# Three seams of a fused graph-convolution and attention kernel: column sums before transposes, extra matmuls at attention's beginning, and two more partial sums on TensorE at its end

## The chip, the cores and the metric

The kernel runs on one core of a Trainium2 chip. Times are device microseconds (us) of a whole execution. The engines are named as in the profile: PE is TensorE's matrix multiplications, PEld its weight loads, DVE is VectorE, ACT is ScalarE, POOL is GpSimd, and SP is the engine that issues most DMAs. "L341" is line 341 of the kernel before.

## The reference

Inputs are `x` (8 graphs x 2048 nodes x 256 features, f32) and one adjacency matrix `adj` (2048 x 2048, f32, with many zeros). Two layers follow each other:

```python
# layer 0: graph convolution, two linear maps, each with a batch norm; residual; layer norm
A = adj + eye
deg  = A.sum(0) + A.sum(1) - diagonal(A)
dinv = rsqrt(deg)
A_hat = A * dinv[:, None] * dinv[None, :]
agg = einsum('nm,bmd->bnd', A_hat, x).reshape(-1, 256)
h   = relu(batchnorm(agg @ W1.T + b1))          # 512 wide, over all 16384 rows
y   = batchnorm(h @ W2.T + b2)                  # 256 wide
x   = layernorm(x + y)
# layer 1: masked attention with 4 heads of 64; residual; layer norm
q, k, v = split(x @ W)
s    = q @ k.T / 8, with -inf where adj == 0
x    = layernorm(x + softmax(s) @ v)
```

All arithmetic stays in f32.

## The kernel before, in words

**Stage 1** reads the adjacency in 16 row tiles `a` of 128 x 2048, in a fixed order of tiles; three buffers hold them. For each tile, PE transposes its sixteen 128 x 128 blocks, four to a PSUM tile `ps` (L234, four buffers); DVE moves three of the four PSUM tiles into the transposed matrix `T` (L240) and ACT the fourth (L238). PE also adds the tile's columns into the PSUM tile `pc` by matrix products with ones (L244), ACT sums its rows (L242), DVE takes its diagonal (L223), and POOL marks the zeros of the diagonal block and adds the identity to it (L249, L250). After the last tile, ACT copies `pc` to `cs` (L261), PE turns `cs` (L264), DVE adds the row and the column sums (L265, L268), and POOL raises the degrees to the power -1/2 in four instructions of four columns each (L99), which gives `dinv`. DVE then makes the first difference of quarters of `T` (`first_t1`, L216 and L217). In this stage DVE, POOL and SP keep the order of the program text (`manual_schedule`); PE and ACT are placed by a planner. In every later stage but a short one all the engines keep the order of the text.

**The first layer.** Products with `T` are made by a recursive scheme with seven products of quarters (`p1` to `p7`) per unit. Each product is eight f32 matrix multiplications, two instructions each (L341). ACT first scales the features of the first unit by `dinv` (L317, 32 instructions), in the order of the halves (0,0), (1,0), (1,1), (0,1); `p1` reads the first, `p2` the last. Then come the linear maps and batch norms (lines 380 to 700).

**Attention's beginning.** The first graph's four chunks of 512 rows get the last batch norm on ACT (`bn`, L764). `ready(c)` transposes such a chunk on PE in two halves into one PSUM tile (`turn_y`, L779, four transposes each); DVE adds the residual (`add_y`, L787) and takes the layer norm's statistics (L728, L730), and POOL makes the roots (`root`, L97, L99, L735, L736). ACT applies the norm (L740), PE turns the result (`turn`, L808), ACT copies it out (L814), and PE projects it to keys and queries (`project`, L845) and values (L859).

**Attention proper.** There are NU = 64 units (a graph, a pair of heads, a chunk of 512 queries) of NT = 16 steps, one for each 128 keys. At step g, PE makes the scores of step g + 3 (L910), DVE masks them (L922), ACT takes the exponential (L928), and PE multiplies those of step g with the values (`weigh`, L940). The softmax's denominators need the sum of all 16 probability tiles `prob` of a unit: POOL adds odd steps to even ones by accumulating DMAs (L950), adds the pairs into `acc` on its own ALU (L959 and L961, five steps after the pair), and PE sums `acc` over its partitions with ones (`finish_sums`, L977). In the last unit the steps 12 to 15 are left to PE as four further `parts`. Small tasks are hung on steps by `at_step(u, j, ...)`: a whole number j runs ahead of the masking of that step, a fraction after it. When the last step is done, what hangs on units NU and NU + 1 runs in order: `finish_sums`, a copy to `sm` (L985), a transpose of it (`finish_turn_sums`, L991, L993, L998), a transpose of the output (`finish_turn`, L1004), the weighting and residual (`finish`, L1012), the final layer norm by halves and the stores (L824). `count_sums` (L1022 to L1028) counts how many of the 8 x 64 sums of each partition are in range; a branch after it (L1255) recomputes everything another way if one is not.

Of the kernel before, what the change touches and what calls it, by code (L numbers as in the profile page):

```python
# [8 lines left out]
F32 = mybir.dt.float32  # L9
U8 = mybir.dt.uint8  # L10
AF = mybir.ActivationFunctionType
ALU = mybir.AluOpType
# [10 lines left out]
SUM_MAX = 1e30  # L23
# [3 lines left out]
def tile_gcn_then_masked_attention(  # L27
# [15 lines left out]
    nc = tc.nc  # L43
    ENG = mybir.EngineType
    PSUM = bass.MemoryType.PSUM
    P = 128
# [8 lines left out]
    CH = 512  # L55
# [142 lines left out]
    with tc.tile_pool(name="bt7", bufs=1, side="right") as bp7, tc.tile_pool(  # L198
        name="stage", bufs=2, side="right"
    ) as sp, tc.tile_pool(name="stage1", bufs=1, side="right") as sp1, tc.tile_pool(  # L200
        name="pst", bufs=4, space=PSUM
    ) as pst, tc.tile_pool(name="psc", bufs=1, space=PSUM) as psc, tc.manual_schedule(
        engines={ENG.SP, ENG.Pool, ENG.DVE}
    ):
        T[1, HALVES[3]] = quarter(7, bp7)
        m8 = bp.tile([P, HT, CH], U8, name="m8")
        rsum = sp1.tile([P, NT], F32, name="rsum")
        diag = sp1.tile([P, NT], F32, name="diag")

        pc = psc.tile([P, CH], F32, name="pc")  # L210
        order = [j * HT + (NK - 1) * TPC + q for j in range(2) for q in range(TPC)]
        order += [j * HT + q for q in range(TPC) for j in range(2)]

        def first_t1(engine, here):
            t1 = T[0, (0, 1)][:, :, here]
            engine.tensor_scalar(m8[:, :, here], t1, 0.0, None, op0=ALU.is_equal)  # L216
            engine.tensor_sub(t1, t1, T[0, (0, 0)][:, :, here])  # L217

        for n, t in enumerate(order):
            a = sp.tile([P, N], F32, name="a", bufs=3)  # L220
            nc.sync.dma_start(a, adj[t * P : (t + 1) * P, :])
# [8 lines left out]
            for g in range(NT // 4):  # L230
# [6 lines left out]
                if g == NT // 4 - 1:  # L237
# [3 lines left out]
            junk = sp1.tile([P, N], U8, name="junk")  # L241
            nc.scalar.activation(junk, a, AF.Copy, accum_out=rsum[:, t : t + 1])  # L242
            for c in range(NCH):
                nc.tensor.matmul(  # L244
                    pc[32 * c : 32 * (c + 1), :], ones[:, :32], a[:, c * CH : (c + 1) * CH],
                    start=(n == 0), stop=(n == NT - 1),
                )
            ad = T[k, (j, j)][:, m, here]
            nc.gpsimd.tensor_scalar(mdiag[:, t, :], ad, 0.0, None, op0=ALU.is_equal)  # L249
            nc.gpsimd.tensor_add(ad, ad, ident)  # L250
            if k == 0 and j == 1 and q < 2:
                first_t1(nc.gpsimd, here)
        for i, j in HALVES:
            S[0, i, j] = load_form(i, j, 0)
        nc.sync.dma_start(w1s, w1t.rearrange("(c p) f -> p c f", p=P))
        for t, src in params:
            nc.sync.dma_start(t, src)
# [3 lines left out]
        nc.scalar.copy(cs, pc)  # L261
# [6 lines left out]
        nc.vector.tensor_add(  # L268
            rsum.rearrange("p (j i) -> p i j", i=TPC),
            pt.rearrange("p i (j r) -> p i j r", j=NCH)[:, :, :, 0],  # L270
            rsum.rearrange("p (j i) -> p i j", i=TPC),
        )
        for q in range(NT // 4):
            qs = slice(q * 4, (q + 1) * 4)
            rsqrt(dinv[:, qs], rsum[:, qs], 4, 0.0)
        first_t1(nc.vector, slice(2 * P, CH))
        mask_out(0, (0, 1), m8)

# [598 lines left out]
    def attention():  # L877


        with tc.tile_pool(  # L880
# [12 lines left out]

            PAIRS = range(0, NT - 2, 2)

            def on_pe(u):
# [46 lines left out]
            def add_up(g):  # L945

                u, j = divmod(g, NT)
                here = NT - on_pe(u)
                if j - 1 in PAIRS and j < here:
                    nc.gpsimd.dma_start(probs[g - 1], probs[g], accum_op=ALU.add)  # L950
                elif PAIRS[-1] + 1 < j < here:
                    nc.gpsimd.tensor_add(accs[u], accs[u], probs[g])  # L952

                v, i = divmod(g - 5, NT)
                if v < 0 or i not in PAIRS[1:] or i + 1 >= NT - on_pe(v):
                    return
                if i == PAIRS[1]:
                    accs[v] = ap_.tile([P, 2, CH], F32, name="acc")
                    nc.gpsimd.tensor_add(accs[v], probs[g - 7], probs[g - 5])  # L959
                else:  # L960
                    nc.gpsimd.tensor_add(accs[v], accs[v], probs[g - 5])  # L961
# [6 lines left out]
            def finish_sums(u):  # L968

                pm = ps_m.tile([P, BR], F32, name="pm")  # L970
                parts = [probs.pop(g) for g in range((u + 1) * NT - on_pe(u), (u + 1) * NT)]
                parts.append(accs.pop(u))
                for n, part in enumerate(parts):
                    for h in range(2):
                        for q in range(2):
                            r0 = 32 * (2 * h + q)
                            nc.tensor.matmul(  # L977
                                pm[r0 : r0 + 32, :], ones[:, :32],
                                part[:, h, q * BR : (q + 1) * BR],
                                start=(n == 0), stop=(n == len(parts) - 1),  # L980
                            )
# [3 lines left out]
                nc.scalar.copy(sts[u], pm)  # L985
# [28 lines left out]
                            op0=ALU.mult, op1=ALU.add,  # L1014
                        )

            def count_sums():

                flat = sums_all.rearrange("p u t h -> p (u t h)")
                ok = ap_.tile([P, CH], F32, name="ot")  # L1020
                cnt = ap_.tile([P, 1], F32, name="cnt", bufs=1)
                nc.vector.tensor_scalar(ok, flat, SUM_MIN, None, op0=ALU.is_ge)  # L1022
                nc.vector.scalar_tensor_tensor(
                    ok, flat, SUM_MAX, ok, op0=ALU.is_le, op1=ALU.mult, accum_out=cnt
                )
                pm = ps_m.tile([1, 1], F32, name="pm")
                nc.tensor.matmul(pm, cnt, ones[:, :1], start=True, stop=True)
# [16 lines left out]
            for u in range(NU):  # L1044
# [11 lines left out]
                elif u == NU - 1:  # L1056
                    for half in range(2):
                        at_step(u + 1, 10.4 + half, inp.emit_stats, b, c, half)
                        at_step(u + 1, 10.5 + half, inp.root_half, b, c, half)
                        at_step(u + 1, 12 + half, inp.emit_half, b, c, half)  # L1060
                    at_step(u + 1, 14, count_sums)
                elif hp == HP - 1:
                    for half in range(2):
                        at_step(u + 1, 12.5 + 1.5 * half, inp.emit_stats, b, c, half)
# [46 lines left out]
            with tc.manual_schedule(engines=IN_ORDER):  # L1111
                for c in range(NCH):
                    inp.yt[0, c] = y0[c]
                    inp.x1[0, c] = ip.tile([P, TPC, D], F32, name="x1", bufs=NCH + 4)
                    for o in range(NO):
                        inp.bn(0, c, o)

                def ready(c):
                    pm = ps_s.tile([P, TPC, D], F32, name="st")
                    for half in range(2):  # L1120
                        pmh = pm[:, half * IT : (half + 1) * IT, :]
                        inp.turn_y(0, c, half, pmh)
                        inp.add_y(0, c, half, pmh, x0[c])
                    inp.root(0, c)

                def halves(f, c):
                    for half in range(2):
                        f(0, c, half)

                for c in range(NCH - 1):  # L1130
                    ready(c)
                halves(inp.apply, 0)
# [168 lines left out]
```

## Time and profile before

| | |
|---|---|
| median of three runs | 3573.38 us (3570.64 to 3573.6) |
| the profiled execution's own time | 3573.89 us |
| its span, first to last instruction | 3571.8 us |
| PE busy | 3524.8 us (99%) |
| POOL busy | 2335.5 us (65%) |
| DVE busy | 2112.7 us (59%) |
| ACT busy | 1575.7 us (44%) |
| mean granted TensorE clock | 0.994 |

The busy times are of one profiled execution. PE is busy in 3524.8 of 3571.8 us, so all its pauses together are 47.0 us; a pause elsewhere that doesn't lengthen one of these, or the time after the last product, is hidden. The granted clock is the speed that TensorE was allowed, 1.0 or 0.5 of the full one in this trace; the records call a slow multiplication just as busy as a fast one.

### The profile page before, as it was taken

The numbers are of one execution on the slowest core, as the hardware profiler recorded it, in microseconds if no ns is written. First come the engines' busy times: TensorE is split into PE (matmuls) and PEld (weight loads), VectorE is DVE, ScalarE is ACT, GpSimd is POOL, SyncE is SP. The second block draws the span as 40 slices with busy tenths as digits, with TensorE's granted clock in tenths as the row PEclk, the third lists the DMA queues.
The fourth block names the chain that finished last, engine by engine and source line by source line (L and its number), as shares of the span: only waits on it lengthen the run. The fifth ranks groups of instructions, "written<-read, shape, count | busy, mean of one in ns | idle before, by whom it ended". The sixth has DMA issues, their size and how long they took to land. (4 is left out here: it accounts for less than half of the span.)

```text
span 3571.8 us, 55309 instructions
## 1 busy us (share of the span) xinstructions
PE 3524.8 (99%) x22447; PEld 1461.9 (41%) x22447; DVE 2112.7 (59%) x3125; ACT 1575.7 (44%) x1952; POOL 2335.5 (65%) x1590
## 2 busy tenths in 40 slices
PE   8999999999999899999999999999999999999997
PEld 5444444444444433433343433343443334343332
DVE  6224342432356656766766776676676676676666
ACT  5000000000045455665665565565566565566555
POOL 4544364435357556777777787777677777777777
PEclk9999999999999899999999999999999999999999
DMA  9122242231256445666575566566556556655555
GB/s 342 53 77 81 90 159 71 71 100 41 77 228 241 152 83 108 129 126 123 111 149 117 115 130 134 110 137 129 114 124 142 110 122 137 120 114 122 113 113 114
DMA packets 197577, 440.16 MB, mean 123 GB/s; under 512 B 14128, under 2 KB 121152, under 8 KB 186944
## 3 DMA queue, kind: packets, MB, share of 16 engines
q0 software_dynamic: 64656, 239.37, 35.3%
q1 hardware_dynamic: 132048, 196.11, 16.0%
q8 instruction: 178, 2.92, 0.3%
q10 hardware_dynamic: 608, 1.06, 0.1%
q14 instruction: 87, 0.71, 0.1%
HBM read 126.62 MB, written 75.51 MB: 57 GB/s over the span
## 5 line engine op out<-in xcount | busy, mean ns | idle before, releaser
L922 DVE SCALAR_TENSOR_TENSOR prob<-mask,st 128x1024 f32<-128x1024 uint8 x1024 | 1239.1, 1215 | 434.5 <-PE st L910 360.6
L928 ACT ACTIVATE prob<-prob 128x1024 f32<-128x1024 f32 x1024 | 1081.2, 1056 | 913.5 <-DVE prob L922 836.3
L940 PE MATMUL out_ps<-prob,v 64*64 64x512 f32 x8192 | 1075.0, 595 | 3.6 <-DVE ot L966 2.6
L910 PE MATMUL st<-qt,kt 64*64 64x512 f32 x8192 | 1063.6, 589 | 0.1
L961 POOL TENSOR_TENSOR acc<-acc,prob 128x1024 f32<-128x1024 f32 x319 | 830.0, 2602 | 5.7 <-DMA prob<-prob 0.7
L341 PE MATMUL pa<-t,x 128*128 128x512 f32 x1792 | 774.5, 594 | 2.7 <-ACT x L317 2.7
L950 POOL DMA_DIRECT2D prob<-prob x447 | 403.8, 929 | 565.3 <-PE out_ps L940 458.0
L910 PEld LDWEIGHTS st<-qt,kt 64*64 64x64 f32 x8192 | 312.6, 133 | 566.7 <-issue 526.9
L341 PEld LDWEIGHTS pa<-t,x 128*128 128x128 f32 x1792 | 342.1, 191 | 431.9 <-issue 427.7
L940 PEld LDWEIGHTS out_ps<-prob,v 64*64 64x64 f32 x8192 | 290.9, 133 | 542.1 <-issue 469.4
L952 POOL TENSOR_TENSOR acc<-acc,prob 128x1024 f32<-128x1024 f32 x126 | 298.1, 2365 | 7.5
L845 PE MATMUL pm<-x1t,wq 128*128 128x512 f32 x512 | 253.0, 617 | 0.7 <-ACT x1t L814 0.7
L470 POOL TENSOR_TENSOR ag<-ag,dbc 128x512 f32<-128x512 f32 x16 | 20.2, 1263 | 314.5 <-DVE ag L469 287.9
L450 ACT COPY ag<-pa 128x512 f32<-128x512 f32 x16 | 9.4, 588 | 448.2 <-PE pa L341 435.1
L399 ACT COPY h<-ph 128x512 f32<-128x512 f32 x28 | 16.4, 585 | 416.7 <-PE ph L390 416.7
L959 POOL TENSOR_TENSOR acc<-prob 128x1024 f32<-128x1024 f32 x64 | 171.1, 2674 | 3.0 <-DMA prob<-prob 3.0
L740 ACT ACTIVATE x<-x,ln_nm,ln_rs 128x256 f32<-128x256 f32 x256 | 137.6, 586 | 8.7 <-POOL ln_nm L736 8.7
L845 PEld LDWEIGHTS pm<-x1t,wq 128*128 128x128 f32 x512 | 87.9, 191 | 119.5 <-issue 112.8
L1012 DVE SCALAR_TENSOR_TENSOR x<-pm,ri,x 128x64 f32<-128x64 f32 x512 | 109.5, 277 | 44.1 <-PE pm L1004 44.1
L859 PE MATMUL pm<-wq,x1t 128*128 128x128 f32 x1024 | 125.1, 276 | 0.0
L859 PEld LDWEIGHTS pm<-wq,x1t 128*128 128x128 f32 x1024 | 119.4, 192 | 2.5 <-ACT x1t L814 1.7
L966 DVE TENSOR_TENSOR ot<-out_ps,ot 128x512 f32<-128x512 f32 x64 | 44.3, 692 | 124.4 <-ACT ot L965 124.4
(156 smaller groups left out, 2855.8 us busy)
## 6 DMA issues: line engine op xcount, KB each, us to landing
prob<-prob POOLq DMA_DIRECT2D x447, 512.0 KB, 4.9
x<-in_x_dram SPq DMA_DIRECT2D x92, 512.0 KB, 6.6
h_d<-h SPq DMA_DIRECT2D x28, 1024.0 KB, 4.2
t<-h_d SPq DMA_DIRECT2D x28, 1024.0 KB, 7.5
a<-in_adj_dram SPq DMA_DIRECT2D x16, 1024.0 KB, 5.0
y_d<-ag SPq DMA_DIRECT2D x32, 512.0 KB, 2.6
out_dram<-x SPq DMA_DIRECT2D x31, 512.0 KB, 6.8
yt<-y_d SPq DMA_DIRECT2D x28, 512.0 KB, 3.2
```

The costliest lines, as they stand in the source:

```text
L341: nc.tensor.matmul(pa, s.t[:, m, :], t[:, m, :], start=(m == 0), stop=(m == HT - 1))
L740: nc.scalar.activation(self.t[:, i, :], self.t[:, i, :], AF.Identity, bias=self.nm[:, i : i + 1], scale=self.rs[:, i : i + 1],)
L845: nc.tensor.matmul(pm, wq[:, d, wcols], xt[:, d, cols], start=(d == 0), stop=(d == ND - 1))
L859: nc.tensor.matmul(pm[:, j * P : (j + 1) * P], xt[:, d, t * P : (t + 1) * P], wq[:, d, wcols], start=(d == 0), stop=(d == ND - 1),)
L910: nc.tensor.matmul(st[r * HD : (r + 1) * HD, h, :], kt[hs, j * P + r * HD : j * P + (r + 1) * HD], qt[hs, cols], start=True, stop=True,)
L922: nc.vector.scalar_tensor_tensor(p, mask[:, j, cols][:, None, :].to_broadcast([P, 2, CH]), MASKED, st, op0=ALU.mult, op1=ALU.add,)
L928: nc.scalar.activation(probs[g], probs[g], AF.Exp)
L940: nc.tensor.matmul(outs[u][hs, r, :], inp.qkv[b, hp][2][rs, j, hs], probs[g][rs, h, :], start=(j == 0), stop=(j == NT - 1),)
L950: nc.gpsimd.dma_start(probs[g - 1], probs[g], accum_op=ALU.add)
L952: nc.gpsimd.tensor_add(accs[u], accs[u], probs[g])
L959: nc.gpsimd.tensor_add(accs[v], probs[g - 7], probs[g - 5])
L961: nc.gpsimd.tensor_add(accs[v], accs[v], probs[g - 5])
```

## The change

It has four parts.

1. **Stage 1.** PE and ACT now keep the order of the text too. The body of the loop is cut into helpers (`turn_a`, `diagonal`, `sum_rows`, `sum_columns`) that hold the same instructions. For the last of the 16 tiles the loop stops after `sum_rows`: its column sums come first, then DVE instead of ACT copies `pc` to `cs`, two of its four groups of transposes stand ahead of the transposes of `cs`, and the other two, with `diagonal`, after the powers. Of the four groups, DVE moves the first and the third, ACT the second and the fourth.
2. **Attention's beginning.** A helper `warm(n)` issues n matrix multiplications of 128 x 512 on PE whose results are not read. Five stand ahead of the first `ready`; one more follows each half's transposes for the chunks 0 and 1.
3. **The last unit's sums.** POOL no longer adds the pairs at steps 8 and 10 into `acc`; PE sums them as two more `parts`, and `acc` is now the first of the parts, not the last.
4. **The range count.** It is made in two: the sums of units 0 to 62 in step 12 of the last unit, the last unit's own after its sums are known. PE adds the two counts with two multiplications, and that (`count_bad`) now stands between the statistics and the root of the first half of the last chunk.

```diff
@@ stage 1
-        engines={ENG.SP, ENG.Pool, ENG.DVE}
+        engines=ALL4
...
+            sum_rows()
+            if n == NT - 1:
+                break
+            for g in range(NT // 4):
+                turn_a(g, g == NT // 4 - 1)
+            sum_columns()
+            diagonal()
             if k == 0 and j == 1 and q < 2:
                 first_t1(nc.gpsimd, here)
+
+        sum_columns()
         for i, j in HALVES:
             S[0, i, j] = load_form(i, j, 0)
...
-        nc.scalar.copy(cs, pc)
+        nc.vector.tensor_copy(cs, pc)
+        turn_a(0, False)
+        turn_a(1, True)
         pt = psc.tile([P, TPC, P], F32, name="pt")
...
             rsqrt(dinv[:, qs], rsum[:, qs], 4, 0.0)
+        turn_a(2, False)
+        turn_a(3, True)
+        diagonal()
         first_t1(nc.vector, slice(2 * P, CH))
@@ last unit's sums
+            LATE = (8, 10)
...
+                if v == NU - 1 and i in LATE:
+                    return
...
-                parts.append(accs.pop(u))
+                if u == NU - 1:
+                    parts = [probs[u * NT + i] for i in LATE] + parts
+                parts.insert(0, accs.pop(u))
@@ range count
+            def count_sums(i):
+                n = TPC * 2
...
+                here = slice((NU - 1) * n, NU * n) if i else slice(0, (NU - 1) * n)
...
+            def count_bad():
                 pm = ps_m.tile([1, 1], F32, name="pm")
-                nc.tensor.matmul(pm, cnt, ones[:, :1], start=True, stop=True)
+                for i in range(2):
+                    nc.tensor.matmul(
+                        pm, cnts[0][:, i : i + 1], ones[:, :1], start=(i == 0), stop=(i == 1)
+                    )
...
-                    at_step(u + 1, 14, count_sums)
+                    at_step(u, 12.8, count_sums, 0)
+                    at_step(u + 1, 10.1, count_sums, 1)
+                    at_step(u + 1, 10.45, count_bad)
@@ attention's beginning
+                def warm(n):
+                    for _ in range(n):
+                        pm = ps_m.tile([P, CH], F32, name="pm")
+                        nc.tensor.matmul(pm, ident, wq[:, 0, :CH], start=True, stop=True)
+
                 def ready(c):
...
                         inp.turn_y(0, c, half, pmh)
+                        if c < 2:
+                            warm(1)
                         inp.add_y(0, c, half, pmh, x0[c])
...
+                warm(5)
                 for c in range(NCH - 1):
                     ready(c)
```

More of the change, by code (lines that the diff above doesn't have):

```diff
@@ L229, in tile_gcn_then_masked_attention, with turn_a @@
             here = slice(q * P, (q + 1) * P)
-            for g in range(NT // 4):
+            def turn_a(g, on_act):
                 ps = pst.tile([P, 4, P], F32, name="ps")
@@ L236, in tile_gcn_then_masked_attention @@
                 dst = T[k, (i, j)][:, m0 : m0 + 4, here]
-                if g == NT // 4 - 1:
+                if on_act:
                     nc.scalar.copy(dst, ps)
@@ L240, in tile_gcn_then_masked_attention, with diagonal, sum_rows, sum_columns @@
                     nc.vector.tensor_copy(dst, ps)
[L241 to L250, printed above, removed]
+            def diagonal():
+                ad = T[k, (j, j)][:, m, here]
+                nc.gpsimd.tensor_scalar(mdiag[:, t, :], ad, 0.0, None, op0=ALU.is_equal)
+                nc.gpsimd.tensor_add(ad, ad, ident)
+            def sum_rows():
+                junk = sp1.tile([P, N], U8, name="junk")
+                nc.scalar.activation(junk, a, AF.Copy, accum_out=rsum[:, t : t + 1])
+            def sum_columns():
+                for c in range(NCH):
+                    nc.tensor.matmul(
+                        pc[32 * c : 32 * (c + 1), :], ones[:, :32], a[:, c * CH : (c + 1) * CH],
+                        start=(n == 0), stop=(n == NT - 1),
+                    )
[6 more added lines that the diff above has]
+            diagonal()
             if k == 0 and j == 1 and q < 2:
                 first_t1(nc.gpsimd, here)
+        sum_columns()
         for i, j in HALVES:
@@ L255, in tile_gcn_then_masked_attention @@
         nc.sync.dma_start(w1s, w1t.rearrange("(c p) f -> p c f", p=P))
-        for t, src in params:
-            nc.sync.dma_start(t, src)
+        for dst, src in params:
+            nc.sync.dma_start(dst, src)
         for s, ij in enumerate(HALVES):
@@ L1015, in finish @@
                         )
[L1017 to L1021, printed above, removed]
+            cnts = []
+            def count_sums(i):
+                n = TPC * 2
+                if not i:
+                    cnts.append(ap_.tile([P, 2], F32, name="cnt", bufs=1))
+                here = slice((NU - 1) * n, NU * n) if i else slice(0, (NU - 1) * n)
+                flat = sums_all.rearrange("p u t h -> p (u t h)")[:, here]
+                ok = ap_.tile([P, CH], F32, name="ot")[:, here]
                 nc.vector.tensor_scalar(ok, flat, SUM_MIN, None, op0=ALU.is_ge)
                 nc.vector.scalar_tensor_tensor(
-                    ok, flat, SUM_MAX, ok, op0=ALU.is_le, op1=ALU.mult, accum_out=cnt
+                    ok, flat, SUM_MAX, ok, op0=ALU.is_le, op1=ALU.mult,
+                    accum_out=cnts[0][:, i : i + 1],
                 )
+            def count_bad():
                 pm = ps_m.tile([1, 1], F32, name="pm")
-                nc.tensor.matmul(pm, cnt, ones[:, :1], start=True, stop=True)
+                for i in range(2):
+                    nc.tensor.matmul(
+                        pm, cnts[0][:, i : i + 1], ones[:, :1], start=(i == 0), stop=(i == 1)
+                    )
                 nc.vector.tensor_scalar(
```

## The prediction

> **What bounds the kernel now.** I read the page first, then the list of who waited for whom on PE, then timelines and tables by stretch of the three places that the change touches. The page's first part:
>
> ```profile
> PE 3524.8 (99%) x22447; PEld 1461.9 (41%) x22447; DVE 2112.7 (59%) x3125; ACT 1575.7 (44%) x1952; POOL 2335.5 (65%) x1590
> ```
>
> PE has only 3571.8 - 3524.8 = 47 us of pauses. Its waits (us in total, times, longest) say where:
>
> ```profile
> PE st L779 <- ACT ag L764: 6.1, 2, 5.9
> PE pc L244 <- DMA a<-in_adj_dram: 5.8, 1, 5.8
> PE st L779 <- DVE x L787: 4.6, 4, 1.5
> PE pm L1027 <- DVE ot L1023: 4.6, 1, 4.6
> PE pm L977 <- POOL acc L961: 3.6, 1, 3.6
> PE pa L341 <- ACT x L317: 2.7, 1, 2.7
> ```
>
> All but the first load lie at the seams being changed. Between 70 and 1220 us PE waits 2.3 us in all, between 1262 and 3515 us 4.2. So what a seam gains in PE's time should arrive at the end.
>
> Busy time doesn't show slow multiplications. The table by stretches does; after the stretch and its length come busy PE, PEld, DVE, ACT, POOL, then the granted clock, DMA share, GB/s:
>
> ```profile
> 53.53:56.94 3.41, 1.24 (x12) 0.42 (x4) 1.70 (x5) 0.80 (x2) 2.07 (x3) 1.00 1.17 297
> 56.94:60.35 3.41, 2.14 (x3) 1.11 (x4) 2.28 (x1) 1.50 (x5) 3.41 (x3) 0.50 0.72 141
> 60.35:63.76 3.41, 3.41 (x5) 1.35 (x5) 0.00 (x0) 3.41 (x13) 3.33 (x5) 0.50 0.96 380
> ...
> 1237.94:1241.35 3.41, 2.74 (x11) 2.04 (x10) 1.73 (x6) 2.02 (x4) 1.71 (x4) 0.50 0.37 118
> 1241.35:1244.77 3.42, 3.42 (x5) 1.35 (x4) 0.00 (x0) 1.52 (x4) 0.44 (x2) 0.50 0.93 320
> 1244.77:1248.18 3.41, 2.63 (x14) 1.51 (x13) 1.34 (x3) 0.79 (x2) 0.00 (x0) 1.00 0.07 23
> ```
>
> The clock halves at 56.94 us, returns at 63.76, halves at 1224.29, returns at 1244.77: whole multiples of 3.41 us apart. A stretch 36% busy (1.24 of 3.41) was followed by half speed; 77% (2.63) kept full speed; 80% (2.74) did not bring it back, a full stretch did. Between 36% and 77% the trace says nothing.
>
> [...] Here a power of four columns (L99) takes 1.0 us alone and up to 2.39 us under L217.
>
> **Part 1, stage 1's end.** The timelines (start, duration) of ACT and of POOL:
>
> ```profile
> 54.18 0.59 ACT L261 COPY cs<-pc 128x512 f32<-128x512 f32 x1 [0.44 <-PE pc L244]
> 57.76 1.28 ACT L317 ACTIVATE x<-x,dinv 128x128 f32<-128x128 f32 x4 [2.99 <-POOL dinv L99]
> 60.13 8.28 ACT L317 ACTIVATE x<-x,dinv 128x128 f32<-128x128 f32 x28 [1.09 <-POOL dinv L99]
> ```
>
> ```profile
> 55.85 6.19 POOL L99 TENSOR_TENSOR dinv<-rsum,mhalf 128x4 f32<-128x4 f32 x4 [0.88 <-DVE rsum L268]
> ```
>
> ACT waits twice for POOL's powers; POOL waits for DVE's L268 (55.51), which had waited for `cs` to be copied and turned. DVE's L217 then runs from 56.93 to 59.22, under the first two powers.
>
> Now the column sums start where the last transposes did, 51.15, and end at 52.22 (1.07). DVE, free at 52.03, copies in 0.63 (three L240 in 1.88) to 52.9. Eight transposes (half of 1.97) fill PE to 53.1; turning `cs` takes 0.66, and POOL starts 0.34 after L268 does: 54.1, not 55.85. DVE's third group (0.63, from 54.2) pushes L216 (1.22) to 54.9 and L217 to 56.1, so the first power runs clear: 55.1 (before: 57.73). The second ends at 56.15 if it just escapes L217, at 58.4 if caught; I take 56.9 (before: 60.08). The stage's first product then starts 0.45 after ACT, near 55.6, not 58.21, and lasts 16 x 0.43 = 6.9 us at full clock, to 62.5. PE's pause shrinks from 2.7 us to some 1.3, which leaves any window about 60% busy: if the clock halves all the same, one window costs 1.7 us (64.2). The second product needs ACT's 25th scaling, 21 x 0.296 = 6.2 us after the second power: 63.2, or 62.4 to 64.7. It started at 67.92: **4.0 us gained** (3.2 to 5.0). Nothing then takes it back: the product that needs the first's PSUM buffer comes at 88.6, so near 84.6, and ACT frees it at 82.15 (81.56 + 0.59, behind stores that don't move).
>
> At nothing I put: transposes ahead of sums for the first tile (the same PE work from 5.77 us on; buffers free within 0.2 us of before); `diagonal` behind the powers (0.53 + 0.46 on POOL; its block is read by DVE after 68 us); DMAs on SP, whose order stays. The loaded features land at 52 to 59 us; the halves used first land before ACT reaches them.
>
> **Part 2, attention's beginning.** PE idles from 1221.8 to 1227.7 waiting for ACT's batch norm, and all until 1244.77 runs at half clock. A filler is two instructions of 0.43 us at full clock; five take 4.3 us of those 5.9. Then DVE paces: 0.63 + 0.75 + 0.30 minus overlap, 1.61 us a half; PE at full clock makes four transposes (0.43) and one filler (0.86) in that, so the filler costs nothing. If the clock stays full, the first four transposes end 0.36 us earlier, DVE's three 0.20 us waits go, and DVE finishes 1.2 us earlier. ACT, held until 1234.7 by a landing store, makes the first norm only 0.4 us earlier; turning it (two halves, 1.92 to 0.86) brings the projection from 1240.56 to 1238.55. Its eight multiplications take 3.4 us, not 5.2: **3.7 us**. But the 1.8 us left idle with the sparse transposes after it make a window as little as 34% busy, and a pause before the projection one of 40%; where the grid falls is chance. One halving leaves about 2.7, two about 1.4. I take **2.7**. If the clock is half throughout, a filler takes 1.71 us and the transposes fall behind: four fillers and five groups of 0.86 end at 1240.2 against 1238.0, **-2.2 us**. Range -2.2 to 3.7.
>
> **Parts 3 and 4, the end.** The timeline:
>
> ```profile
> 3550.17 1.93 PE L977 MATMUL pm<-prob,ones 128*32 128x256 f32 x32
> ...
> 3550.88 4.78 POOL L961 TENSOR_TENSOR acc<-acc,prob 128x1024 f32<-128x1024 f32 x2
> ...
> 3555.71 1.08 PE L977 MATMUL pm<-acc,ones 128*32 128x256 f32 x8 [3.61 <-POOL acc L961]
> 3556.91 0.37 ACT L985 COPY sm<-pm 128x256 f32<-128x256 f32 x1 [3.40 <-PE pm L977]
> ```
>
> The two late POOL additions go. `acc` is complete at 3546.85, the last accumulating DMA has landed by 3549.5 (no traffic after), so PE sums seven parts without a wait: 7 x 0.48 = 3.4 us from 3550.17 to 3553.6, not 3556.8. What is late next is ACT: the previous unit's norm waits for POOL's root[...], about 0.6 us longer. ACT then does two pairs (1.09 each) and `ot` (0.56) from 3551.6 to 3554.1, before `sm`: 2.8 us gained. After it, full clock saves 0.25 us on L991 and more on L1004; the small count adds 0.5 and `bad` 0.2 to DVE. POOL's last roots lose the contention with the old count (L736 0.46 for 0.20, L97 0.68 for 0.24): 0.7 saved. The last norm starts at 3561.3, not 3564.8: **3.4 us** (2.6 to 4.0). The branch reads a count that is ready earlier still; the last store ends the run as before.
>
> **Sum.** 4.0 + 2.7 + 3.4 = 10.1 us. From the profiled execution's 3573.9 that gives 3563.8; the median of the runs shown is 0.5 lower, 3573.4, so 3563.3. I say 3563.5.
>
> **Rivals.**
> - *The clock isn't held.* Part 2 gives 1 us, part 1 3.3, the end 3: 3566.6 from the profiled time. For it: windows of 34% to 60%, below the 77% seen to hold. Against it: the fillers fill DVE's pauses.
> - *Layer 0 gives part 1 back*, by a wait on something timed by DMA (the buffer above, 2.4 us of margin): 3573.9 - 6.1 = 3567.8. Against it: PE's 2.3 us of waits in 1150.
> - *The fillers delay the transposes* at half clock: 3573.9 - 4.0 + 2.2 - 3.4 = 3568.7. Against it: fillers plus cold transposes fill whole windows, which brings the clock back.
> - *Slower: ACT paces stage 1.* In fixed order the fourth copy stands behind `sum_rows` (1.91 + 0.19). If PE waited for all of that at each of 15 tiles, it would cost 31.5 us: 3595.3. It makes the kernel slower from 10.1 / 15 = 0.7 us a tile, by 0.2% from 1.15. Against it: ACT already goes in this order from the third tile on, and waits 0.41 us a tile for PE; a tile is 2.69 us of ACT and 2.89 of PE.
>
> **How the numbers follow.** Some 0.2% (7.1 us) can be told from no change. The forecast has 0.66, the first rival 0.12 (half of it within 0.2%), the second 0.09, the third 0.07, the slower one 0.04, something unnamed within 0.2% 0.02. So faster 0.72, same 0.24, slower 0.04. The low end is all best cases, 5.0 + 3.7 + 4.0 = 12.7 under 3573.4; the high end takes in rivals two and three: 3560.7 to 3569.0.
>
> **What would show it.** Right: L99 starts near 54.1, the second product near 63 to 64.5; full clock in some of 1224 to 1245; no L961 after 3547 less the shift; L985 about 2.8 us nearer to the last step. Wrong: PE waits in layer 0 that grow by microseconds, L341 still at half clock until after 60, fillers late enough that DVE waits for L779 longer than 0.2 us, or L985 waiting for a DMA.

## The result, and the profile after

| | before | after |
|---|---|---|
| median | 3573.72 us (3570.64 to 3574.88, 12 runs) | 3564.30 us (3562.31 to 3566.12, 12 runs) |
| profiled execution | 3573.89 us | 3566.12 us |
| its span | 3571.8 us | 3564.3 us |

The ratio is 0.9975 (95% interval 0.9967 to 0.9984): 9.4 us faster, where 10.1 were forecast, 3564.3 us where 3563.5 were. The near hit hides that one part gave about a quarter of its share and another more than its share. The profiled execution of after happens to be the slowest of its twelve, so the traces differ by 7.8 us and the medians by 9.4; what probably makes up the rest is found below. Two runs, 4618.38 us of `part3_only` and 3840.76 us of the kernel before in the same group, were slow, at a granted clock of 0.75 and 0.91, and are left out of the ratios below.

The page's first part, of the kernel after, and the list of PE's waits (us in total, times, longest):

```profile
PE 3527.1 (99%) x22483; PEld 1461.0 (41%) x22483; DVE 2113.4 (59%) x3128; ACT 1575.4 (44%) x1952; POOL 2330.5 (65%) x1588
```

```profile
PE ps L235 <- DMA a<-in_adj_dram: 7.3, 4, 6.0
PE pa L363 <- ACT t L239: 2.8, 1, 2.8
...
PE out_ps L963 <- DVE ot L991: 2.6, 3, 1.0
PE st L801 <- DVE x L809: 2.3, 3, 1.2
PE pa L633 <- POOL x L628: 2.1, 3, 1.3
PE st L801 <- ACT ag L786: 2.0, 2, 1.6
```

The waits for batch norm (6.1 us, L764 then, L786 now), for `acc` (3.6) and for the count (4.6) have shrunk or gone, as the prediction had it. But the wait ahead of stage 1's first product is as long as before, 2.8 us for 2.7; only the releaser has another name: a copy into `T` (L239) instead of the scaled features. PE's pauses are 3564.3 - 3527.1 = 37.2 us, 9.8 fewer, while 36 more instructions run.

**Stage 1's end** in the trace of after, ACT's timeline, then one line each of POOL's, DVE's and PE's (start, duration, engine, line):

```profile
57.63 0.70 ACT L339 ACTIVATE x<-x,dinv 128x128 f32<-128x128 f32 x2 [2.19 <-POOL dinv L99]
58.23 0.57 ACT L239 COPY t<-ps 128x512 f32<-128x512 f32 x1
```

```profile
55.67 6.13 POOL L99 TENSOR_TENSOR dinv<-rsum,mhalf 128x4 f32<-128x4 f32 x4 [1.02 <-DVE rsum L287]
```

```profile
56.34 1.22 DVE L216 TENSOR_SCALAR m<-t 128x2048 uint8<-128x2048 f32 x1
```

```profile
58.90 10.16 PE L363 MATMUL pa<-t,x 128*128 128x512 f32 x16 [2.76 <-ACT t L239]
```

The copy of the last tile's fourth group runs *behind* two scalings, which wait for POOL's first power. The change meant ACT to keep the order of the text here, and the text has the copy first (`turn_a(3, True)` stands ahead of L339); in the kernel as built ACT does not. Why is not shown. PE has finished that group at 56.1; ACT, idle from 55.44, could have copied it two microseconds before it did. The first product starts at 58.90 (before: 58.21), at half clock for two windows, from 58.27 to 65.10. (A window is one of the stretches of 3.41 us at whose edges, the grid of the prediction, the clock changed in these traces.) The table by stretches there (busy PE, PEld, DVE, ACT, POOL, then clock, DMA share, GB/s):

```profile
54.86:58.27 3.41, 1.27 (x12) 1.03 (x10) 2.99 (x6) 1.22 (x4) 2.60 (x2) 0.99 1.16 294
58.27:61.68 3.41, 2.78 (x4) 1.26 (x5) 1.69 (x1) 3.41 (x13) 3.41 (x3) 0.50 0.84 184
```

**Attention's beginning**, PE's timeline:

```profile
1222.61 4.45 PE L1163 MATMUL pm<-wq,ident 128*128 128x512 f32 x10
1228.67 0.33 PE L801 MATMUL st<-ident,ag 128*128 128x128 f32 x1 [1.61 <-ACT ag L786]
...
1239.29 3.70 PE L867 MATMUL pm<-x1t,wq 128*128 128x512 f32 x8 [0.73 <-ACT x1t L836]
1242.82 0.60 PE L801 MATMUL st<-ident,ag 128*128 128x128 f32 x4
```

The five fillers take 4.45 us of the pause and leave 1.61; the granted clock is 1.00 in every stretch from 1215 to 1250 us; the projection takes 3.70 us for 5.78. From the first transposes to the fourth chunk's it is 14.15 us, for 18.46 before.

**The end**, ACT's timeline:

```profile
3548.12 1.09 ACT L762 ACTIVATE x<-x,ln_nm,ln_rs 128x256 f32<-128x256 f32 x2 [2.34 <-POOL ln_nm L758]
3549.12 0.56 ACT L990 COPY ot<-out_ps 128x512 f32<-128x512 f32 x1
3549.59 1.09 ACT L762 ACTIVATE x<-x,ln_nm,ln_rs 128x256 f32<-128x256 f32 x2
3550.58 0.35 ACT L1012 COPY sm<-pm 128x256 f32<-128x256 f32 x1
```

PE sums the seven parts from 3546.85 without a wait and is done at 3550.08; the copy to `sm` then stands behind ACT's norm, as forecast. Last multiplications with values begin at 3545.83 (3549.15 before), so everything ahead has brought 3.32 us; measured from there `sm` is copied 3.0 us sooner and the last norm, at 3557.22, starts 4.28 us sooner.

### The profile page after: what moved, and what is told of

It reads as the page before. It is cut to its first block, busy times and chain, and to the rows that moved or that the text cites. A ratio compares the mean times of both kernels' runs of the same rounds, so it can differ in the third digit from the quotient of the medians.

```text
span 3564.3 us, 55375 instructions
## 1 busy us (share of the span) xinstructions
PE 3527.1 (99%) x22483; PEld 1461.0 (41%) x22483; DVE 2113.4 (59%) x3128; ACT 1575.4 (44%) x1952; POOL 2330.5 (65%) x1588
## 3 DMA queue, kind: packets, MB, share of 16 engines
q10 hardware_dynamic: 608, 1.06, 0.1%
## 5 line engine op out<-in xcount | busy, mean ns | idle before, releaser
L945 DVE SCALAR_TENSOR_TENSOR prob<-mask,st 128x1024 f32<-128x1024 uint8 x1024 | 1239.0, 1215 | 434.6 <-PE st L933 358.6
L421 ACT COPY h<-ph 128x512 f32<-128x512 f32 x28 | 16.4, 585 | 416.7 <-PE ph L412 416.7
L1039 DVE SCALAR_TENSOR_TENSOR x<-pm,ri,x 128x64 f32<-128x64 f32 x512 | 109.6, 277 | 43.6 <-PE pm L1031 43.6
L991 DVE TENSOR_TENSOR ot<-out_ps,ot 128x512 f32<-128x512 f32 x64 | 44.3, 692 | 123.9 <-ACT ot L990 123.9
```

The source lines that it names most:

```text
L945: nc.vector.scalar_tensor_tensor(p, mask[:, j, cols][:, None, :].to_broadcast([P, 2, CH]), MASKED, st, op0=ALU.mult, op1=ALU.add,)
```

## The experiments

Each kernel shared the runs of the kernel before with those sent along with it; "before" below is the median of those runs. The kernel after was not run again with them: its 3564.30 us is from its own twelve runs. As the medians of before moved from 3572.96 to 3573.72 between the groups, a difference from after of less than some 0.8 us is not shown by the times alone.

**Theory.** Parts 2 and 3 do what the prediction says; part 1's gain is caught by ACT's fourth copy behind the scalings. **Rivals:** stage 1 is slower in itself because all its engines now keep the order of the text; the clock, not the copy, takes the gain; the parts hinder each other.

**One part at a time.** Each kernel is the one before with one part of the diff shown above, and all else as it was.

```diff
 # part1_only: these, and the helpers they need
-        engines={ENG.SP, ENG.Pool, ENG.DVE}
+        engines=ALL4
-        nc.scalar.copy(cs, pc)
+        nc.vector.tensor_copy(cs, pc)
+        turn_a(0, False)
...
```

> The kernel before with part 1 (stage 1) alone. Theory A (each seam pays for itself, and part 1 pays little): the changed kernel's trace shows its second product starting 1 us later than before, because the first product waits for ACT's last copy and the clock halves in the pause; where the clock's grid falls better it is 2 us earlier. So between +1 and -2 us, near 0. Theory B (part 1 gives the 4 us that the prediction put on it, and the trace was an unlucky one): about -4 us.

Measured: 3570.72 us (3569.14 to 3575.43) against 3572.96, ratio 0.9995 (0.9987 to 1.0003). 2.2 us by the medians, not told apart from nothing. The 4.0 us did not come. In its trace, too, the first product waited 2.76 us for the copy of L239; this profiled execution was the slowest of the thirteen.

```diff
 # part2_only
+                        if c < 2:
+                            warm(1)
...
+                warm(5)
```

> The kernel before with part 2 (the filling multiplications at attention's beginning) alone. Theory A: the trace shows the projection's last results 3.35 us earlier although everything started 0.96 us later, so -4.3 us if the clock stays full, and -2 to -3 if it halves once. Theory B (the fillers hold up the transposes and the gain comes from elsewhere): 0 to +2 us.

Measured: 3569.74 us (3569.0 to 3570.77), ratio 0.9990 (0.9982 to 0.9999): 3.2 us. The runs now lie within 1.8 us. Of the 49 runs of the kernel before in this group 48 fall on two levels, about 3571.3 and 3574.3 us. In traces without fillers, first to fourth chunk takes either 18.5 us (before, and part 1 alone) or 16.4 (parts 3 and 4 alone), with fillers 14.15. Of the 2.9 us between the levels, 2.1 then stand in this stretch, where the clock stays at half for six windows in the first two traces and for four in the others. With fillers the stretch is 4.3 us shorter than in the worse case.

```diff
 # part3_only
+                if v == NU - 1 and i in LATE:
+                    return
...
+                if u == NU - 1:
+                    parts = [probs[u * NT + i] for i in LATE] + parts
+                parts.insert(0, accs.pop(u))
```

> The kernel before with part 3 (the last unit's two late pairs summed by PE, acc first) alone. Theory A: the copy of the sums no longer waits for POOL's two additions but for PE's seven parts and ACT's two norms; without the range count beside POOL's root nothing delays these, so -3.1 to -3.5 us. Theory B (the wait passes to ACT or a DMA): -1 us or less.

Measured: 3567.93 us (3566.83 to 3570.54), ratio 0.9988 (0.9981 to 0.9995): 5.0 us by the medians, of which some belongs to the levels. The trace gives it without them: from the last multiplications with values, `sm` is copied 3.39 us sooner and the last norm starts 3.97 us sooner than before.

```diff
 # part4_only
-                    at_step(u + 1, 14, count_sums)
+                    at_step(u, 12.8, count_sums, 0)
+                    at_step(u + 1, 10.1, count_sums, 1)
+                    at_step(u + 1, 10.45, count_bad)
```

> The kernel before with part 4 (the range count in two) alone. Theory A: POOL's last roots lose the contention with the long count (0.7 us), the small count and the bad cell add 0.2 to 0.5 us to DVE's chain: -0.2 to -0.7 us, which five rounds can hardly tell from nothing. Theory B (the branch at the end waits for the count): -1 us or more.

Measured: 3573.23 us, ratio 1.0001 (0.9993 to 1.0009): nothing that the times show. The trace has the last norm 0.63 us sooner, close to what the prediction gave the last roots. Parts 3 and 4 alone would make 4.60 us of the last norm; together they made 4.28. A likely reason is that the early count slows POOL's root (L99 1.45 us for 1.04) ahead of the norm that `sm` waits behind; in part 4 alone `sm` waited for `acc`, not for that norm.

```diff
 # without_part1: the kernel after with stage 1 as before
-        engines=ALL4
+        engines={ENG.SP, ENG.Pool, ENG.DVE}
...
```

> The changed kernel without part 1 (stage 1 as before), parts 2 to 4 kept. Theory A (part 1 pays about 2 us, the median of part 1 alone): 7 to 7.5 us under the kernel before, so 2 us slower than the changed kernel's 9.4. Theory B (part 1 pays nothing, all comes from the other two seams, whose traces show 4.3 each): 8.5 to 9.5 us under the kernel before.

Measured: 3565.38 us (3564.71 to 3567.1), ratio 0.9978 (0.9970 to 0.9987), against 3564.30 of after. By these medians part 1 pays 1.1 us in company, about a quarter of its forecast; by what each kernel gained on the runs of before sent with it, 1.7 (9.4 - 7.75). That lies between the two theories and decides for neither.

**What takes part 1's gain?** The next three kernels change the kernel after in stage 1 alone.

```diff
 # last_group_on_dve
         turn_a(2, False)
-        turn_a(3, True)
+        turn_a(3, False)
```

> The changed kernel with the last tile's fourth group moved by DVE, not by ACT. Theory A (the first product waits for ACT's copy behind the first two scalings, and the first power is held until L216 ends, 1.9 us for 1.0): DVE's extra copy pushes L216 behind the first power, which takes 1.0 to 1.2 us; the first product starts 3 us after the last transposes' begin or less, near 57.2 on the scale of the changed kernel's trace where it began at 58.9: 1.5 us faster than the changed kernel, more where the clock is kept. Theory B (the powers hold it, whatever DVE does): within 0.3 us of the changed kernel, and a first power of 1.9 us.

Measured: 3561.30 us (3560.82 to 3562.08), ratio 0.9967 (0.9955 to 0.9979), 3.0 us less than after. Its timelines of ACT and of PE, and the stretch that holds the pause:

```profile
56.02 1.28 ACT L339 ACTIVATE x<-x,dinv 128x128 f32<-128x128 f32 x4 [1.31 <-POOL dinv L99]
57.51 2.74 ACT L339 ACTIVATE x<-x,dinv 128x128 f32<-128x128 f32 x9 [0.21 <-POOL dinv L99]
```

```profile
56.47 7.13 PE L363 MATMUL pa<-t,x 128*128 128x512 f32 x16 [1.06 <-ACT x L339]
63.44 0.27 PE L324 MATMUL ph<-ident,dinv 128*16 128x128 f32 x1
63.80 6.71 PE L363 MATMUL pa<-t,x 128*128 128x512 f32 x15
```

```profile
54.66:58.07 3.41, 2.35 (x11) 1.38 (x10) 3.09 (x5) 1.89 (x7) 3.12 (x3) 1.00 1.16 298
```

POOL's powers and DVE's L216 there:

```profile
54.95 5.75 POOL L99 TENSOR_TENSOR dinv<-rsum,mhalf 128x4 f32<-128x4 f32 x4 [0.94 <-DVE rsum L287]
```

```profile
56.22 1.22 DVE L216 TENSOR_SCALAR m<-t 128x2048 uint8<-128x2048 f32 x1
```

The copy is out of ACT's way; the pause is 1.06 us for 2.76; no window falls to half clock there (1.00 after one that is 69% busy, 2.35 us), and the first product takes 7.13 us for 10.16. The second starts at 63.80, 4.2 us sooner than in the kernel before (68.03). Two things came together, the shorter pause and the full clock. There is a second effect, as large as the first: DVE's L216 now stands behind two copies (1.29 us) and starts 1.27 us after POOL's first power, not 0.67, so that this power takes 1.04 us for 1.93 in after. Counted from the start of that power the first product comes 1.7 us sooner than in after: 0.9 of it is the shorter power, and 0.8 that no copy stands between ACT's first scaling and the product (0.45 us from one to the other for 1.27). The edit brings both, and no kernel has one without the other.

```diff
 # last_group_on_dve_and_filler
-        turn_a(3, True)
+        turn_a(3, False)
+        hold = pst.tile([P, CH], F32, name="ps")
+        nc.tensor.matmul(hold, ident, a[:, :CH], start=True, stop=True)
```

> As last_group_on_dve, and one multiplication of 128 x 512 whose result is not read, on PE after the last transposes. Theory A (the clock halves because windows around the pause are 43% busy or less): the first product's sixteen instructions take 6.9 us and not 8.5 to 10.2; the second product is then held by ACT's scalings to about 64.7 (69.0 in the changed kernel's trace): 3 to 4 us faster than the changed kernel. Theory B (the clock halves elsewhere or the filler delays the product): no more than last_group_on_dve gives.

Measured: 3561.60 us (3561.19 to 3562.72), ratio 0.9968 (0.9956 to 0.9980), as without the filler; first product from 56.32, 7.11 us. The clock stayed full without the filler (pause 1.06 us) as with it (0.28). Pause and clock are not parted by this pair, since no kernel kept the long pause and held the clock. The traces give the shares: the product starts 1.7 us sooner, and it is 1.7 us shorter than with one window at half clock (8.80 us, below), 3.0 shorter than with two. In stage 1 every trace with the long pause (2.74 or 2.76 us) has the half clock in the first product (8.54 to 10.16 us), and none with a short one (0.28 to 1.07 us, products of 7.11 or 7.13 us), so it is taken as the pause's consequence.

```diff
 # old_placing: the kernel after, ACT and PE placed by the planner again
-        engines=ALL4
+        engines={ENG.SP, ENG.Pool, ENG.DVE}
```

> The changed kernel with PE and ACT of stage 1 placed by the planner again, as before, all else as changed. Theory A (the fixed order costs 0.9 us over stage 1, because the first tile's sums, read last, free its buffer 0.8 us later): 0.5 to 1 us faster than the changed kernel, its first load into a freed buffer issued near 10.4 and not 11.2. Theory B (that delay is chance, the kernel before also differs by 1 us from run to run): within 0.4 us, or slower where the planner puts the last column sums behind the transposes.

Measured: 3563.82 us (3563.38 to 3564.51), ratio 0.9973 (0.9963 to 0.9984), 0.5 us less than after. The transposes of `cs` start at 53.95 us for 54.65, but PE waits for L239 just as long, 2.76 us, and ACT has the copy behind the same two scalings. So the placing is not where the missing 3 us are. Whether it costs some tenths is not shown: in the five traces with the old stage 1, one and the same text, that mark ranges from 54.82 to 56.22. Its first product took 8.80 us, one window at half clock, where the profiled execution of after had two (10.16). The two kernels of the next group, whose stage 1 is that of after, also show 8.80, and their second products start at 67.22 and 67.16 where after's profiled execution has 69.01. That fits the 1.8 us by which this execution lies over after's median (3566.12 - 3564.30).

The theory thus named one of two causes, the copy, and not the held power. Of the rivals, the first is too small to explain the loss, and the second is part of the same event. For the third, the four parts alone sum to 10.2 us (2.2 + 3.2 + 5.0 - 0.3) against 9.4 together, a difference that the scatter covers.

**Which fillers hold the clock?**

```diff
 # no_leading_fillers
-                warm(5)
 # no_fillers_between
-                        if c < 2:
-                            warm(1)
```

> The kernel after without the five fillers ahead of the first chunk's transposes; the one filler a half in chunks 0 and 1 stays. Theory (the pause for batch norm is itself what halves the clock): PE idles some 5 us again, the first transposes run at 0.86 us a group and the interior fillers at 1.7, the interval from the first transposes to the fourth chunk's grows from 14.15 to 16 us or more, and the kernel takes 2 to 4 us more than after (3566 to 3568). Rival (the interior fillers alone bring the clock back within a window or two): up to 1 us more (3564.3 to 3565.3).

Measured: 3565.25 us (3563.23 to 3566.59), ratio 0.9975 (0.9966 to 0.9984), 0.95 us more than after, at the edge of the rival's span and within the scatter. First to fourth chunk took 16.19 us for 14.15: PE waited 5.90 us for batch norm, the clock halved in that pause, near 1226.1, and with the fillers between it was back after two windows, near 1233.0.

> The kernel after without the filler of each half in chunks 0 and 1; the five ahead of them stay. Theory (DVE paces the halves, PE is busy only some 30% of a half without fillers, so the windows there lie under the 38% that dropped elsewhere): the clock halves once inside, the fourth chunk's transposes come 1 to 3 us later than 14.15 us after the first, the kernel takes 1 to 3 us more than after (3565.3 to 3567.3). Rival (transposes and DVE's pace keep it, the five alone did the work): within 0.4 us of after, 3564.

Measured: 3568.09 us (3564.32 to 3570.41), ratio 0.9985 (0.9979 to 0.9992), 3.8 us more than after, more than the theory said. In its trace the clock halves at 1229.36, after the leading fillers had held it, and stays so for four windows:

```profile
1225.95:1229.36 3.41, 1.37 (x9) 0.95 (x10) 1.21 (x3) 3.07 (x5) 0.00 (x0) 1.00 0.61 240
1229.36:1232.77 3.41, 1.79 (x10) 1.39 (x9) 3.34 (x12) 2.79 (x4) 1.14 (x2) 0.50 0.97 338
1232.77:1236.18 3.41, 1.90 (x9) 1.50 (x8) 3.14 (x11) 2.07 (x4) 1.75 (x5) 0.50 0.00 1
1236.18:1239.59 3.41, 2.73 (x12) 2.24 (x11) 1.93 (x8) 1.82 (x4) 1.65 (x5) 0.50 0.33 105
1239.59:1243.00 3.41, 3.41 (x5) 1.35 (x4) 0.00 (x0) 1.51 (x4) 0.63 (x3) 0.50 0.89 311
```

PE (the first figure after the length) is busy for 1.37 us, 40%, in the window ahead of the drop, and only the projection at its end fills a whole window. First to fourth chunk took 17.69 us here. So the four fillers between the halves are worth more than the five ahead of them: 3.8 us against 0.95 by the medians, 3.5 against 2.0 in the traces. The runs range over 6 us, so how much is lost varies from run to run.

**A better version.** Two kernels go on from `last_group_on_dve`.

```diff
 # dve_group_and_tail
-                        at_step(u + 1, 14 + half, inp.emit, b, c, half)
+                    at_step(u + 1, 14, inp.emit, b, c, 0)
+                    at_step(u + 2, 7, inp.emit, b, c, 1)
 # dve_group_tail_old_placing: this, and
-        engines=ALL4
+        engines={ENG.SP, ENG.Pool, ENG.DVE}
```

> Last tile's fourth group copied by DVE (as in last_group_on_dve), and the second half of the last unit but one's stored norm on ACT put behind the copy of the last unit's sums. Theory (ACT sets the tail: the copy of the sums stands behind that norm, 3549.59 to 3550.58, while PE was done at 3550.08): the copy comes 0.5 us earlier, the last norm 0.4 to 0.5 earlier, 3560.8 against last_group_on_dve's 3561.3. Rival (the norm only moves behind the copy and delays ot's or the roots' ACT work by as much, or the last stores): no difference or up to 0.5 slower, 3561.3 to 3561.8.

Measured: 3562.01 us (3560.53 to 3562.38), ratio 0.9966 (0.9954 to 0.9978). ACT's timeline at its end:

```profile
3545.15 0.56 ACT L990 COPY ot<-out_ps 128x512 f32<-128x512 f32 x1
3546.24 0.37 ACT L1012 COPY sm<-pm 128x256 f32<-128x256 f32 x1 [0.52 <-PE pm L1004]
3546.51 1.09 ACT L762 ACTIVATE x<-x,ln_nm,ln_rs 128x256 f32<-128x256 f32 x2
```

The copy comes at 3546.24 for 3546.60 in `last_group_on_dve` (the step before it, 3515.49 for 3515.47, shows the two traces level), the last norm 0.33 us sooner. ACT now waits for PE, so this is all that the swap can give. The times, 0.7 us apart the other way with ranges that overlap, don't show it: inconclusive.

> As dve_group_and_tail, with stage 1's ACT and PE instructions placed by the planner again, as before the change (the order of SP, POOL and DVE stays as written). Theory (the fixed order on ACT and PE costs the 0.7 us by which the last tile's transposes come later): 0.5 us less than dve_group_and_tail, 3560.3. Rival (with DVE's copy the seam is paced by POOL's roots and the planner puts ACT's row sums of the last tile ahead of something needed): equal or slower, 3560.8 to 3563.

Measured: 3560.75 us (3560.45 to 3561.1), ratio 0.9963 (0.9949 to 0.9977), the fastest of all: 3.5 us under after, 12.8 under before. The transposes of `cs` start 1.06 us sooner than in the kernel just above and the first product 1.05 (55.44 for 56.49), about as much as the times differ. That suggests that the order of the text on ACT and PE costs about one microsecond here, but does not show it: the ranges overlap, and the same mark moves by 1.4 us between traces whose stage 1 is the same.

## Why the prediction was right and wrong

**Part 1: 4.0 us forecast, 1.1 to 1.7 measured in company, 2.2 alone.** The prediction's own signs say the same: L99 started at 55.67, not near 54.1, the second product at 69.0, not near 63 to 64.5, and the first was at half clock until after 60, which it had named as a sign of being wrong. By the steps of its working:

- "Now the column sums start where the last transposes did, 51.15": they start near 52.87. Stage 1 itself ran late: the transposes of the last tile but one stand at 49.97 us for 48.26. This mark moves without any change: it lies from 48.26 to 49.66 in the five traces with the old stage 1, of which the prediction had the earliest, and from 49.01 to 50.03 in the seven with part 1 in the order of the text. So part of the lateness may be chance and part that order, which the prediction put at nothing; they were not isolated. From there to the first power it takes 2.8 us, for the 2.95 forecast.
- "so the first power runs clear: 55.1": it escaped L217 but not L216 (56.34 to 57.56), and took 1.93 us; with L216 1.27 us behind its start, in `last_group_on_dve`, it took 1.04. The prediction reckoned with a longer power beside L217 alone. The trace of before could have told: its first power, from 55.85 to 57.72, took 1.9 us, though the last one there, with DVE idle, takes 1.00 and L217 began only at 56.93. What ran beside it at first was L216, in DVE's timeline of before:

```profile
55.61 1.22 DVE L216 TENSOR_SCALAR m<-t 128x2048 uint8<-128x2048 f32 x1
```

- "The stage's first product then starts 0.45 after ACT." It took ACT's *scaling* as the last thing awaited, and did not ask what else the product reads. It reads the last tile's fourth group, which had moved behind the powers; in ACT's built order two scalings stand ahead of that copy, though the text has it sooner. So the product starts 1.27 us after ACT. In all it starts at 58.90, not 55.6: 1.6 us from the late start of the powers, 0.9 from the held power, 0.8 from this copy. The last two also lengthen the pause, to 2.76 us where the prediction had 1.3, and leave the window 37% busy where it had some 60%; the clock halved as well. With that copy on DVE the second product starts at 63.80, where the prediction had 63.2, and the kernel is 4.1 us under the one without part 1 (3565.38 - 3561.30): the forecast's size was right for a kernel that was not the one built. (Its 4.0 us is not 67.92 - 63.2, which is 4.7, but lies towards the case with a window at half clock; and at 67.92 stands a small product ahead of the second one, which started at 68.03.) As built, the second product starts near 67.2 where one window was at half clock and at 69.0 where two were, against 67.74 to 68.46 in the five traces with the old stage 1: that fits a gain of about 1 us.

**Part 2: 2.7 forecast, 3.2 measured alone.** It went as reckoned: DVE paces (PE still waits for L809 three times, 2.3 us), the fillers cost nothing, the projection is faster (3.70 us for 5.78). The low windows did not halve the clock in the trace of after (the lowest 45% busy, 1.53 of 3.41 us from 1235.87), so it shows 4.3, above even the 3.7 that the working gave for a full clock throughout: counted from the first transposes the projection starts 2.23 us sooner, where 2.0 were reckoned, and the stretch from its start to the fourth chunk is 2.08 us shorter, where 1.8 were. Which windows between 36% and 77% keep the full clock it could not know; the runs show some of them, below. Where the grid falls, which it called chance, does differ between traces of one text: with the old stage 1 the clock halved from 1.3 us before the first product's start (before) to 0.1 after it (`part4_only`).

**Parts 3 and 4: 3.4 forecast, 4.28 in the trace.** ACT was late next, and `sm` came 3.0 us sooner where 2.8 were forecast. Beside the early count POOL's root took 0.4 us longer (L99 1.45 us for 1.04), where the author's estimate was 0.6. The mis-sized term is the stretch from `sm` to the weighting (L1039): 1.45 us for 2.01 before, a gain of 0.56. The prediction set 0.25 us saved on L991, and an amount on L1004 that it did not give, against 0.5 for the small count; in its sum of 3.4 that leaves 0.1. That count's two instructions took 0.12 and 0.17 us. The last roots gave 0.7, as forecast.

**The sum** of 10.1 against 9.4 was near in part by luck: part 1's shortfall of about 2.9 was half made good by the other two (0.5 and 0.9), for reasons that its working did not have. The other part is not accounted for; that the median of before was 3573.72, not the 3573.4 reckoned with, is 0.3 of it. Of the rivals, the clock's came true at stage 1's end and not at attention's beginning. The others did not happen: layer 0 took nothing back (at 1211 us POOL's L628 stands 0.96 us later than before, and the second product had stood 0.98 later), the fillers delayed nothing, ACT did not pace stage 1's tiles.

On the held power: L216 reads one tile (`m<-t`), L217 two (`t<-t,t`). The first power ended with L216, 1.93 us for 1.04; L216 moved its 2048 values a partition in 1.22 us where L217 needed 2.29. What it is in either that makes a power longer no run here shows. Transposes and fillers ran in the order of the text: in the trace of after the five fillers (1222.61, 4.45 us) stand ahead of the first transposes (1228.67), and each later filler (1.02 us) follows the four transposes of its half.

## What to carry to other kernels

When the wait ahead of an instruction is shortened, list all that the instruction reads and look up, in each producer's built order, what stands in front: the next latest input sets the gain. Look as well at what will run beside an instruction once it moves: here that cost as much (0.9 us beside L216, and 0.8 by the copy). A pause need not be filled wholly for a gain: here 1.61 us stayed open behind the five fillers, and the clock was full in the trace of after, though `last_group_on_dve` with the same 1.61 us lost a window. Four fillers between the halves were worth more than a block of five ahead of them (3.8 us against 0.95 by the medians). Where times of the kernel before fall on two levels, compare marks within the traces, beside the medians.

## What the hardware showed that was not expected

- Which windows kept the clock at these seams. Windows 36% busy (before), 37% (after) and 40% (`no_fillers_between`) were followed by half speed, and so was one of 42% in `last_group_on_dve` at attention's beginning, 1.42 of 3.41 us. Three windows later in the same trace one of 48% kept full speed, and in `dve_group_and_tail` one of 45% did:

```profile
1221.78:1225.19 3.41, 1.42 (x7) 0.72 (x6) 0.79 (x4) 2.47 (x4) 0.32 (x1) 1.00 0.87 274
1225.19:1228.60 3.41, 3.41 (x9) 1.77 (x8) 2.94 (x10) 1.35 (x3) 0.00 (x0) 0.50 1.04 392
```

```profile
1231.89:1235.30 3.41, 1.53 (x12) 1.29 (x12) 3.34 (x12) 2.26 (x6) 1.73 (x4) 1.00 0.00 0
1235.30:1238.72 3.42, 3.38 (x8) 1.58 (x9) 0.32 (x3) 2.54 (x5) 1.70 (x4) 1.00 0.89 289
```

  So at attention's beginning 42% was followed by half speed and 45% was not, in these traces. PE's busy share alone does not sort the windows: at the end of `old_placing` one 53% busy, with sums whose weights are 128 x 32 (L1004) and a few transposes, was followed by half speed:

```profile
3547.50:3550.91 3.41, 1.80 (x22) 0.94 (x14) 2.03 (x11) 1.47 (x4) 0.00 (x0) 1.00 0.35 125
3550.91:3554.33 3.42, 0.00 (x0) 0.00 (x0) 2.56 (x14) 0.77 (x2) 2.04 (x6) 0.50 0.10 34
```

- Full speed also came back after a window that was not full. One of 80% (2.74 us, before) stayed at half speed, as the prediction read, but one of 83% (2.82 us) in `part3_only` was followed by full speed:

```profile
1237.15:1240.56 3.41, 2.82 (x12) 2.42 (x12) 2.81 (x10) 1.28 (x3) 1.72 (x4) 0.50 0.13 18
1240.56:1243.97 3.41, 3.09 (x7) 1.44 (x8) 0.00 (x0) 2.83 (x6) 1.48 (x3) 1.00 0.96 328
```

- All four kernels with the fourth group's copy on DVE lost one window at attention's beginning: first to fourth chunk took 15.27 us for 14.15, so about 1.1 us is left there. The five leading fillers of `last_group_on_dve` ended 1.6 us before the first transposes. Why all four fell so is not shown, and one or two more fillers there were not tried.
- The runs of the kernel before differ by some 3 us, in two levels (about 3571.3 and 3574.3 us), without any change of the program.
